# First attention of a two-layer kernel: the last products of a block in four pieces among the next block's scores and transposes, and the queries scaled by ScalarE

## The chip, the cores and the metric

The kernel runs on one core of one Trainium2 chip. The metric is the device time of one execution in microseconds; the figure to beat is the median of three runs.

## What is computed

There are two layers, each an attention and a mixture of experts, on x of shape (4, 512, 256) in float32. The change touches only the first attention of layer 0. For each of the four batches ("blocks" here), with e the layer-normed rows of x, q the 1024 context rows, and w1, w2, w3 thirds of a weight vector, it is

```
Sim  = (e @ w1)[:, None] + (q @ w2)[None, :] + (e * w3) @ q.T + b
A    = softmax(Sim, axis=1)                 # 512 x 1024
hq   = A @ q                                # 512 x 256
Batt = softmax(max(Sim, axis=1), axis=0)
hc   = Batt @ e                             # one row of 256, the same for all rows
x   += concat([e, hq, e * hq, e * hc]) @ W_qv + b_qv
```

After it come, per block, the routing of the 512 rows to the experts (a layer norm, logits, the two best experts, a place for each row, indirect stores of the rows), then the experts' tiles, then layer 1. The kernel computes (e * w3 + w2) @ q.T in one product, and leaves out what a softmax cancels.

## The kernel before, in words

**Tiling.** A block's 512 rows are four tiles t of 128 rows. `sim_norm` is the layer norm (VectorE, and one square root on ScalarE). `sim_prep` (L273) transposes the normed rows with TensorE into two PSUM tiles `eTp` (one for each half c of the 256 columns), copies each to `eT`, and makes the scaled queries `q0T`. `sim_scores(t)` (L297) makes a 128x1024 score tile `s` in PSUM with L301, its negated row maximum on VectorE (L307), the exponential on ScalarE into `p` (L251), and the division by the row sum on VectorE (L253, L254). `turn_probs(t)` (L257) transposes `p` in eight pieces into two PSUM tiles `a0t` (L261); VectorE copies the first to `a0T` (L265), ScalarE the second (L267).

**The end of a block.** `sim_finish` is a generator in pieces. `attend(0)` and `attend(1)` are the products `hq` over `a0T` (L331), each evicted by ScalarE (`hqT`, L334) and then VectorE (`ehT`, L335). Then comes the row `hc` (L350, L352), and the products of W_qv with `hqT` and `ehT` for tiles 0 and 1 (`hcq`, L367). Its last piece turns the row `hc` (`hcc`, L379), builds the weights `weff` from it on VectorE (L385), does the products with `weff` for the four tiles, those of tiles 2 and 3 together with their `hqT` and `ehT` products, and adds each tile to x on VectorE (L392).

**Order.** TensorE runs the program order, written out by hand in `layer0_attention`: while block b is finished, the scores and transposes of block b+1, the preparation of block b+2 and the routing of block b-1 (`route_steps`: norm L784 to L804, transposes L235, logits `lgT` L834, `lg` L843 and the choice of experts up to `rt_cnt` L852, places `pos` L860 and L861 up to `rt_posi` L874, stores `rows` L894) are put between the pieces. The order on VectorE, ScalarE and GpSimd is chosen by a planner when the kernel is built; each engine then runs its own list in order.

**Buffers.** Three PSUM pools hold two buffers each: score tiles, transposes (`ps_t`: `eTp`, `a0t`, `g`, `hc`, `hcc`, `gb` and others), products (`ps_m`: `hq`, `hcq`, `lgT`, `lg`, `pos`, `k`, `v`). A buffer is written again only after its last reader. In SBUF the pool `k4` has twelve buffers of 4 KB per partition, for `xn`, `eT`, `q0T`, `p`, `hqT`, `ehT` and others. Its first tile is `zeros`, the source of nine transfers that clear the buffers in DRAM (20.6 MB written), issued by GpSimd (L194 and L201).

**After the attention.** TensorE goes on with keys and values of layer 1 (`k` L475, `v` L489) while block 3 is routed (its normed rows are `rowbuf`), and then with the experts' tiles.

Of the kernel before, what the change touches and what calls it, by code (L numbers as in the profile page):

```python
# [12 lines left out]
AF = mybir.ActivationFunctionType  # L13
ALU = mybir.AluOpType
# [3 lines left out]
P = 128  # L18
NB = 4
S = 512  # L20
NT = S // P
M = 1024
NJ = M // P
D = 256
# [36 lines left out]
def two_layers(ctx: ExitStack, tc: tile.TileContext, io, out):  # L61
# [75 lines left out]
    def after(a, b, why):  # L137
        info = mybir.DependencyInfo(mybir.DependencyClass.Sync, mybir.DependencyReason.DATA)
        tc.add_manual_dep(a.ins, b.ins.name, info, reason=why)
# [10 lines left out]
    x = []  # L150
# [3 lines left out]
    def load_ctxn(b):  # L154
        t = t8([P, NJ, D], f"ctxn_{b}")
        nc.sync.dma_start(out=t, in_=io["ctx"][b].rearrange("(j p) d -> p j d", p=P))
        ctxn[b] = t
# [98 lines left out]
    def turn_probs(dst, p, t, name):  # L256

        for g in range(2):
            pt = tr_ps(f"{name}_{g}")
            for j in range(4):  # L260
                nc.tensor.transpose(pt[:, bass.ts(j, P)], p[:, bass.ts(4 * g + j, P)], ident)  # L261
            d = dst[:, 4 * g : 4 * g + 4, bass.ts(t, P)]
            s = pt.rearrange("p (j n) -> p j n", n=P)
            if g == 0:
                nc.vector.tensor_copy(d, s)  # L265
            else:
                nc.scalar.copy(d, s)  # L267
# [5 lines left out]
    def sim_prep(st):  # L273
        b, xn = st["b"], st["xn"]
        eT = t4([P, NC, S], f"eT_{b}")
        qT = t4([P, NC, S], f"q0T_{b}")
        for c, pt in transposed(xn, f"eTp_{b}"):
            nc.vector.tensor_copy(eT[:, c, :], pt)
            st["scaled"] = nc.vector.tensor_scalar(  # L279
                qT[:, c, :], eT[:, c, :], wsim[:, 2, c : c + 1], wsim[:, 1, c : c + 1], ALU.mult, ALU.add  # L280
            )
        nc.gpsimd.tensor_tensor(x[b], x[b], bqv.unsqueeze(1).to_broadcast([P, NT, D]), ALU.add)
        st.update(eT=eT, qT=qT, negmax=tsmall([P, NT], "s0_negmax"))

    def sim_rows(st):
# [10 lines left out]
    def sim_scores(st, t):  # L296
        b = st["b"]  # L297
        sp = score_ps(f"s0_{b}_{t}")
        for c in range(NC):
            for h in range(2):  # L300
                nc.tensor.matmul(  # L301
                    sp[:, h, :], st["qT"][:, c, bass.ts(t, P)], ctxT[b][:, c, bass.ts(h, 512)],
                    start=(c == 0), stop=(c == NC - 1),
                )
        spf = sp.rearrange("p h n -> p (h n)")
        nm = st["negmax"][:, t : t + 1]
        nc.vector.tensor_reduce(nm, spf, AX.X, ALU.max, negate=True)  # L307
        p = t4([P, M], f"p0_{b}_{t}")
        softmax_exp(p, spf, 1.0, nm)
        return p  # L310

    def sim_finish(st):

        b, xn, eT, aT = st["b"], st["xn"], st["eT"], st["aT"]

        mx = tsmall([P, NT], "b0_mx")
        nc.vector.scalar_tensor_tensor(mx, st["r"], bsim, st["negmax"], ALU.add, ALU.subtract)
        m1 = tsmall([P, 1], "b0_m1")
        nc.vector.tensor_reduce(m1, mx, AX.X, ALU.max)
        gp = tr_ps(f"g0_{b}")  # L320
        nc.tensor.transpose(gp[0:1, 0:P], m1, ident)
        g = tsmall([1, 1], "b0_g")
        nc.vector.tensor_reduce(g, gp[0:1, 0:P], AX.X, ALU.max, negate=True)

        hq = t4([P, NC, S], f"hqT_{b}")
        eh = t4([P, NC, S], f"ehT_{b}")

        def attend(c):
            op = mm_ps(f"hq_{b}_{c}")
            for j in range(NJ):  # L330
                nc.tensor.matmul(  # L331
                    op, ctxn[b][:, j, bass.ts(c, P)], aT[:, j, :], start=(j == 0), stop=(j == NJ - 1)
                )
            nc.scalar.copy(hq[:, c, :], op)  # L334
            st["attended"] = nc.vector.tensor_tensor(eh[:, c, :], op, eT[:, c, :], ALU.mult)  # L335

        attend(0)
        yield
        bp = tr_ps(f"gb0_{b}")
        nc.tensor.matmul(bp[:, 0:1], ones[0:1, :], g, start=True, stop=True)  # L340
        gb = tsmall([P, 1], "b0_gb")
        nc.vector.tensor_copy(gb, bp[:, 0:1])
        eb = tsmall([P, NT], "b0_eb")
        es = tsmall([P, 1], "b0_es")
        nc.scalar.activation(eb, mx, AF.Exp, bias=gb, accum_out=es)
        attend(1)
        yield

        hp = tr_ps(f"hc0_{b}")
        nc.tensor.matmul(hp[0:1, D : D + 1], es, ones[:, 0:1], start=True, stop=True)  # L350
        for t in range(NT):
            nc.tensor.matmul(  # L352
                hp[0:1, 0:D], eb[:, t : t + 1], xn[:, t, :], start=(t == 0), stop=(t == NT - 1)
            )
        rt = tsmall([1, 1], "b0_rt")
        nc.vector.reciprocal(rt, hp[0:1, D : D + 1])
        hr = sm.tile([1, D], F32, tag="b0_hr", name=f"b0_hr_{b}", bufs=1)
        nc.vector.tensor_scalar(hr, hp[0:1, 0:D], rt, None, ALU.mult)
        ops = {}

        def products(t, k, last):
            if not last:
                ops[t] = mm_ps(f"hcq_{b}_{t}")[:, 0:D]
            op = ops[t]
            for c in range(NC):
                for i, (l, w) in enumerate(k):
                    nc.tensor.matmul(  # L367
                        op, l[:, c, bass.ts(t, P)], w(c), start=(not last and c == 0 and i == 0),
                        stop=(last and c == NC - 1),
                    )  # L370

        late = [(hq, lambda c: wqv[:, 2 + c, :]), (eh, lambda c: wqv[:, 4 + c, :])]
        for t in range(2):
            products(t, late, False)
        yield

        hp = tr_ps(f"hcc0_{b}")
        for c in range(NC):
            nc.tensor.matmul(hp[:, c : c + 1], hr[:, bass.ts(c, P)], ones[0:1, 0:1], start=True, stop=True)  # L379
        hc = tsmall([P, NC], "b0_hc")  # L380
        nc.vector.tensor_copy(hc, hp[:, 0:NC])

        weff = sm.tile([P, NC, D], F32, tag="weff", name=f"weff_{b}", bufs=1)
        for c in range(NC):
            nc.vector.scalar_tensor_tensor(  # L385
                weff[:, c, :], wqv[:, 6 + c, :], hc[:, c : c + 1], wqv[:, c, :], ALU.mult, ALU.add
            )
        for t in range(NT):
            if t >= 2:
                products(t, late, False)  # L390
            products(t, [(eT, lambda c: weff[:, c, :])], True)
            nc.vector.tensor_tensor(x[b][:, t, :], ops[t], x[b][:, t, :], ALU.add)  # L392

        yield

    def layer0_attention():


        st, ps = {0: sim_norm(0)}, {}

        def scores(b, t):
            ps[t] = sim_scores(st[b], t)

        def turns(b, t):
            if t == 0:
                st[b]["aT"] = tbig(f"a0T_{b}")
            turn_probs(st[b]["aT"], ps.pop(t), t, f"a0t_{b}_{t}")

        def step():
            if route is not None:  # L410
                next(route)

        sim_prep(st[0])
        st[1] = sim_norm(1, st[0]["scaled"])
        load_ctxn(1)
        scores(0, 0)
        scores(0, 1)
        sim_rows(st[0])
        turns(0, 0)
        scores(0, 2)  # L420
        turns(0, 1)
        scores(0, 3)
        sim_prep(st[1])
        turns(0, 2)
        turns(0, 3)
        route = None
        for b in range(NB):
            more = b + 1 < NB
            fin = sim_finish(st[b])
            next(fin)  # L430
            if b + 2 < NB:
                st[b + 2] = sim_norm(b + 2, st[b]["attended"])
            step()
            if more:
                scores(b + 1, 0)
            next(fin)
            step()
            if more:
                scores(b + 1, 1)
            next(fin)  # L440
            if more:
                turns(b + 1, 0)
            next(fin)
            step()
            if more:
                sim_rows(st[b + 1])
                scores(b + 1, 2)
                turns(b + 1, 1)
                scores(b + 1, 3)
                if b + 2 < NB:  # L450
                    load_ctxn(b + 2)
                    sim_prep(st[b + 2])
            step()
            if more:
                turns(b + 1, 2)
                turns(b + 1, 3)
            route = route_steps(L0, b)
            next(route)
        return route
# [941 lines left out]
```

## Time and profile before

| | us |
|---|---|
| median of 3 runs | 987.43 (987.35 to 987.92) |
| profiled execution, whole | 984.93 |
| span of the profiled execution | 982.9 |
| TensorE busy | 902.5 (92%) |
| VectorE busy | 439.6 (45%) |
| ScalarE busy | 328.7 (33%) |
| GpSimd busy | 227.1 (23%) |
| mean granted TensorE clock | 0.971 of full speed |

The first attention with its routing fills about the first 246 us of the span. The profile's lines read: start, length, engine, line of the kernel, operation, output and inputs by the program's names, count, and in brackets the idle time of that engine just before, with what released it. TensorE's ends are modelled, so that the starts are the safer numbers.

### The profile page before, as it was taken

What the parts mean: (1) busy time and instruction counts of PE and PEld (TensorE: products, weight loads), DVE (VectorE), ACT (ScalarE), POOL (GpSimd) and SP (SyncE); (2) the same over time, 40 slices, a digit from 0 to 9 for tenths busy, and PEclk for the clock granted to TensorE, in tenths of its full rate; (3) what the DMA queues carried; (4) which work ended last, traced back from release to release, by engine and by line L of the source; (5) the groups of instructions that cost most, each with busy time, mean ns of one, the idle gap of its engine ahead of it and who ended that gap; (6) DMA issues with size and microseconds to landing.
All of it is one profiled execution on the core that took longest, in us unless ns stands there. A gap on an engine that the chain in (4) does not pass through costs nothing.

```text
span 982.9 us, 15181 instructions
## 1 busy us (share of the span) xinstructions
PE 902.5 (92%) x5506; PEld 672.3 (68%) x5506; DVE 439.6 (45%) x1262; ACT 328.7 (33%) x727; POOL 227.1 (23%) x275
## 2 busy tenths in 40 slices
PE   5888999988989999989989989989899999999995
PEld 2445464645569899546656655656778999999995
DVE  6455474544732322665664765756461211112110
ACT  2222221221111111365673464555332322323321
POOL 3310103040512222000130141133642112221121
PEclk9898999989999999999999999999989999999998
DMA  9999901211139797600000111220325868578971
GB/s 317 288 259 236 284 2 34 84 51 43 46 93 303 227 298 272 222 22 2 23 1 1 29 49 62 90 98 23 108 81 150 277 198 270 175 238 269 292 243 19
DMA packets 54907, 142.05 MB, mean 145 GB/s; under 512 B 6775, under 2 KB 32814, under 8 KB 48681
## 3 DMA queue, kind: packets, MB, share of 16 engines
q1 hardware_dynamic: 39144, 102.89, 31.4%
q0 software_dynamic: 15392, 38.10, 15.2%
q8 instruction: 47, 0.77, 0.3%
q14 instruction: 36, 0.29, 0.1%
q10 hardware_dynamic: 288, 0.00, 0.0%
HBM read 131.51 MB, written 39.91 MB: 174 GB/s over the span
## 4 chain that ended last, share of the span: by engine, by line
PE 46%; DVE 4%; ACT 4%; issue 4%; DMA 1%; another core or an unknown queue 0%; POOL 0%; POOLq 0%; ACTq 0%; DVEq 0%
PE hp L1085 11%; PE y L1110 10%; PE s L587 6%; PE a2t L610 5%; PE o L635 4%; DVE p L596 2%; ACT p L600 2%; PE y_ahead L1110 2%; PE hp_ahead L1085 1%; DMA out<-yw,to 1%; PE q L571 1%; PE v L489 1%; PE k L475 1%; PE b L934 1%; PE lgT L834 1%
## 5 line engine op out<-in xcount | busy, mean ns | idle before, releaser
L1094 ACT ACTIVATE aT<-hp,w1s 128x128 f32<-128x128 f32 x248 | 67.6, 383 | 159.2 <-issue 159.2
L1085 PEld LDWEIGHTS hp<-hT,w1s 128*128 128x128 f32 x992 | 115.6, 192 | 3.5 <-DVE hT L1066 1.9
L1085 PE MATMUL hp<-hT,w1s 128*128 128x128 f32 x992 | 116.2, 275 | 1.4 <-DVE hT L1066 1.4
L1110 PE MATMUL y<-w2s,aT 128*128 128x256 f32 x496 | 112.0, 379 | 0.0
L596 DVE CUSTOM_DVE_ANT_0 p<-s,mbias 128x1024 f32<-128x1024 f32 x64 | 75.8, 1221 | 54.0 <-PE s L587 53.9
L1110 PEld LDWEIGHTS y<-w2s,aT 128*128 128x128 f32 x496 | 91.9, 190 | 11.2
L600 ACT ACTIVATE p<-p,s_nm 128x1024 f32<-128x1024 f32 x64 | 73.5, 1148 | 66.1 <-DVE s_nm L596 66.1
L1127 POOL DMA_INDIRECT out<-yw,to x31 | 47.8, 1542 | 178.2 <-DVE to L1051 90.6
L610 PEld LDWEIGHTS a2t<-ident,p 128*128 128x128 f32 x512 | 56.9, 143 | 44.9 <-issue 22.1
L1114 DVE TENSOR_SCALAR yw<-y,row 128x256 f32<-128x256 f32 x59 | 28.6, 484 | 125.4 <-PE y L1110 125.4
L610 PE MATMUL a2t<-ident,p 128*128 128x128 f32 x512 | 72.8, 283 | 12.2 <-ACT a2T L615 5.8
L894 POOL DMA_INDIRECT rows<-rowbuf,rt_posi x64 | 65.2, 1019 | 77.5 <-DVE rt_posi L874 19.7
L587 PE MATMUL s<-kT,q2T 64*128 64x512 f32 x256 | 68.9, 642 | 2.1 <-DVE s_nm L596 2.1
L635 PE MATMUL o<-a2T,v 128*64 128x128 f32 x1024 | 63.3, 276 | 1.7 <-ACT kT L480 1.1
L331 PE MATMUL hq<-a0T,ctxn 128*128 128x512 f32 x128 | 63.0, 649 | 0.5 <-DVE a0T L265 0.5
L635 PEld LDWEIGHTS o<-a2T,v 128*64 128x64 f32 x1024 | 55.4, 137 | 11.5 <-issue 7.5
L615 ACT COPY a2T<-a2t 128x512 f32<-128x512 f32 x96 | 53.7, 581 | 23.0 <-PE a2t L610 22.7
L301 PE MATMUL s<-ctxT,q0T 128*128 128x512 f32 x128 | 59.8, 613 | 0.5 <-DVE q0T L279 0.5
L1066 DVE TENSOR_SCALAR hT<-ht,w1s 128x128 f32<-128x128 f32 x62 | 22.6, 406 | 81.7 <-PE ht L1060 76.0
L1085 PEld LDWEIGHTS hp<-hT,w0s 128*128 128x128 f32 x448 | 54.2, 192 | 3.3 <-DVE hT L1062 2.0
L1085 PE MATMUL hp<-hT,w0s 128*128 128x128 f32 x448 | 54.8, 276 | 1.1 <-DVE hT L1062 1.0
L1110 PE MATMUL y<-w0s,aT 128*128 128x256 f32 x224 | 52.8, 379 | 0.0
(259 smaller groups left out, 1245.7 us busy)
## 6 DMA issues: line engine op xcount, KB each, us to landing
w1s<-in_w1p SPq DMA_DIRECT2D x34, 1030.0 KB
w2s<-in_w2p SPq DMA_DIRECT2D x34, 1024.0 KB
rows<-zeros POOLq DMA_DIRECT2D x8, 2064.0 KB
w0s<-in_w1p SPq DMA_DIRECT2D x31, 512.0 KB
w0s<-in_w2p SPq DMA_DIRECT2D x31, 512.0 KB
row<-rows SPq DMA_DIRECT2D x59, 129.0 KB
ctxT<-in_ctxT SPq DMA_DIRECT2D x4, 1024.0 KB
ctxn<-in_ctx SPq DMA_DIRECT2D x4, 1024.0 KB
```

What stands on the lines that cost most here:

```text
L301: nc.tensor.matmul(sp[:, h, :], st["qT"][:, c, bass.ts(t, P)], ctxT[b][:, c, bass.ts(h, 512)], start=(c == 0), stop=(c == NC - 1),)
L331: nc.tensor.matmul(op, ctxn[b][:, j, bass.ts(c, P)], aT[:, j, :], start=(j == 0), stop=(j == NJ - 1))
L587: nc.tensor.matmul(sps[r][:, k, :], st["qT"][at, n, bass.ts(t, P)], st["kT"][at, n, bass.ts(k, 512)], start=True, stop=True,)
L596: nc.vector.tensor_tensor_reduce(p, sps[r].rearrange("p h n -> p (h n)"), st["mbias"][:, t, :], -ATT_SCALE, -ATT_SCALE * LEAST, ALU.add, A ...
L600: nc.scalar.activation(p, p, AF.Exp, bias=nm, scale=-1.0, accum_out=tot[:, r : r + 1])
L610: nc.tensor.transpose(pt[:, bass.ts(j, P)], p[:, bass.ts(4 * g + j, P)], ident)
L615: nc.scalar.copy(d, pt)
L635: nc.tensor.matmul(op[r * HD : r * HD + HD, :], st["v"][:, j, bass.ts(2 * n + r, HD)], aT[:, r, bass.ts(j, P)], start=(j == 0), stop=(j == ...
L894: i = nc.gpsimd.indirect_dma_start(out=rows[:, :], out_offset=bass.IndirectOffsetOnAxis(ap=pos_i[:, k, t : t + 1], axis=0), in_=buf[:, k, ...
L1085: nc.tensor.matmul(o, w1[:, c * ff + f * P : c * ff + f * P + P], hT[:, c, :], start=(c == 0), stop=(c == NC - 1),)
L1094: nc.scalar.activation(aT[:, f, :], hp[:, f // 4, bass.ts(f % 4, P)], AF.Gelu_apprx_tanh, bias=w1[:, at : at + 1])
L1110: nc.tensor.matmul(op, aT[:, f, :], w2[:, f * D : f * D + D], start=(f == 0), stop=(f == nf - 1))
```

## The change

In `sim_prep` the scaled queries are made by ScalarE from the PSUM tile, not by VectorE from `eT`; GpSimd's addition of b_qv to x now comes after the last of these. In `sim_finish` the last piece becomes four: the row and the weights `weff`; the final products of tiles 0 and 1; those of tile 2; those of tile 3. In `layer0_attention` the scores of block 1's tile 0 come before block 0's last transposes; in every block the scores (b+1, 2) come between the piece that makes `weff` and the first final products; the transposes (b+1, 1) and the scores (b+1, 3) come before the products of tiles 2 and 3; and the preparation of block b+2 and the transposes (b+1, 2) come after these.

```diff
         for c, pt in transposed(xn, f"eTp_{b}"):
-            nc.vector.tensor_copy(eT[:, c, :], pt)
-            st["scaled"] = nc.vector.tensor_scalar(
-                qT[:, c, :], eT[:, c, :], wsim[:, 2, c : c + 1], wsim[:, 1, c : c + 1], ALU.mult, ALU.add
+            st["scaled"] = nc.vector.tensor_copy(eT[:, c, :], pt)
+            scaled = nc.scalar.activation(
+                qT[:, c, :], pt, AF.Identity, bias=wsim[:, 1, c : c + 1], scale=wsim[:, 2, c : c + 1]
             )
-        nc.gpsimd.tensor_tensor(x[b], x[b], bqv.unsqueeze(1).to_broadcast([P, NT, D]), ALU.add)
+        i = nc.gpsimd.tensor_tensor(x[b], x[b], bqv.unsqueeze(1).to_broadcast([P, NT, D]), ALU.add)
+        after(i, scaled, "not beside VectorE's copies")
...
                 weff[:, c, :], wqv[:, 6 + c, :], hc[:, c : c + 1], wqv[:, c, :], ALU.mult, ALU.add
             )
+        yield
         for t in range(NT):
...
             nc.vector.tensor_tensor(x[b][:, t, :], ops[t], x[b][:, t, :], ALU.add)
-
-        yield
+            if t > 0:
+                yield
...
         turns(0, 2)
+        scores(1, 0)
         turns(0, 3)
...
             step()
-            if more:
+            if more and b > 0:
                 scores(b + 1, 0)
...
             next(fin)
+            if more:
+                scores(b + 1, 2)
+            next(fin)
             step()
             if more:
                 sim_rows(st[b + 1])
-                scores(b + 1, 2)
                 turns(b + 1, 1)
                 scores(b + 1, 3)
-                if b + 2 < NB:
-                    load_ctxn(b + 2)
-                    sim_prep(st[b + 2])
+            next(fin)
+            next(fin)
+            if b + 2 < NB:
+                load_ctxn(b + 2)
+                sim_prep(st[b + 2])
+            if more:
+                turns(b + 1, 2)
             step()
             if more:
-                turns(b + 1, 2)
                 turns(b + 1, 3)
```

One consequence for the routing: `step()`, which for b > 0 runs a piece of the routing of block b-1, keeps its place after the piece that holds tiles 0 and 1. So `lg` and the choice of experts of block b-1 now come before the products of tiles 2 and 3, and `pos` after them. For the last block nothing of a next block stands between the pieces.

More of the change, by code (lines that the diff above doesn't have):

```diff
@@ L401, in scores @@
         def scores(b, t):
-            ps[t] = sim_scores(st[b], t)
+            ps[b, t] = sim_scores(st[b], t)
         def turns(b, t):
@@ L406, in turns @@
                 st[b]["aT"] = tbig(f"a0T_{b}")
-            turn_probs(st[b]["aT"], ps.pop(t), t, f"a0t_{b}_{t}")
+            turn_probs(st[b]["aT"], ps.pop((b, t)), t, f"a0t_{b}_{t}")
         def step():
```

## The prediction

> **What bounds the kernel now.** I read the page's busy shares first: TensorE is busy 92% of the span, so idle TensorE is what can be won. Its slices:
>
> ```profile
> PE   5888999988989999989989989989899999999995
> PEclk9898999989999999999999999999989999999998
> DMA  9999901211139797600000111220325868578971
> ```
>
> The first ten slices (246 us) hold the first attention. There TensorE has idle tenths and the granted clock dips, while DMA is full until slice 5. The chain of waits reaches back only to 396 us, to the end of the first experts, so it says nothing of this stage. I therefore took the timeline of TensorE, in order of time, and looked for waits:
>
> ```profile
> 72.12 3.68 PE L367 MATMUL hcq<-weff,eT 128*128 128x256 f32 x8 [3.37 <-DVE weff L385]
> ...
> 129.84 1.99 PE L367 MATMUL hcq<-weff,eT 128*128 128x256 f32 x8 [0.77 <-DVE weff L385]
> ...
> 203.68 1.06 PE L261 MATMUL a0t<-ident,p 128*128 128x128 f32 x8 [2.89 <-DVE p L254]
> ...
> 206.27 10.06 PE L331 MATMUL hq<-a0T,ctxn 128*128 128x512 f32 x16 [0.47 <-DVE a0T L265]
> ...
> 245.31 0.42 PE L860 MATMUL pos<-rt_cnt,before 128*128 128x48 f32 x2 [3.87 <-DVE rt_cnt L852]
> ```
>
> TensorE waits for `weff` in each block (0.77 us; 3.37 in block 0, where GpSimd adds to x at 69.33), for the last `p` of block 3, and for the choice of experts. After a longer wait the work itself is slow: the 10.06 us of `hq` are 7.03 at 151.79. The windows show why:
>
> ```profile
> 205.28:208.70 3.42, 2.81 (x4) 0.51 0.15 54
> 208.70:212.10 3.40, 3.40 (x5) 0.50 0.23 80
> 246.24:249.65 3.41, 3.41 (x5) 0.51 0.00 0
> ```
>
> Columns: window, length, TensorE busy (count), granted clock, DMA. The clock is half for one or two windows of 3.41 us.
>
> One thing in this stage is not bound by TensorE. The exponential of tile 1 of block 2:
>
> ```profile
> 121.77 1.23 DVE L307 TENSOR_REDUCE s_negmax<-s 128x1 f32<-128x1024 f32 x1 [2.89 <-PE s L301]
> ...
> 124.51 1.11 ACT L251 ACTIVATE p<-s,s_negmax 128x1024 f32<-128x1024 f32 x1 [7.60 <-DVE s_r L291]
> ```
>
> Its maximum was done at 123.0, yet it began at 124.51. The order of ScalarE, in both kernels, lists all eight GpSimd DMA semaphores at this instruction: its `p` gets the buffer of `zeros`, so **it waits until the clearing transfers have landed**. DMA share falls from 0.42 (121 to 122 us) to 0.07 in the next us.
>
> [...] clock 0.50, all changes on a grid of 3.41 us, and windows with 1.55 us of work or less were followed by half clock (89.23 to 92.64), one with 2.19 (147.25) was not. [...] `ehT` at 47.83 starts as `hqT` ends (47.80). So `q0T` on ScalarE waits for VectorE's copy of the same bank; the order of waits of the changed kernel shows it. [...] no table load stands before `q0T` in the new order.
>
> **The change part by part.** The orders of both kernels show that after the first attention all five engines' lists are the same, so what TensorE gains by 246 us should pass to the end unless a transfer is bound to absolute time.
>
> *Queries on ScalarE.* Removes 8 scalings from VectorE (0.55 us at 9.77), adds 8 on ScalarE; priced by the eviction `hqT` of the same shape, 0.59. VectorE's copy still comes first (0.69), so the first scores start at 10.37 as before; at each later `eTp` the buffer is free 0.6 us later than by the copy alone. The bounds of the unseen instruction are 0.59 and 0.7. GpSimd's additions come after ScalarE: block 1's now behind the clears in its queue, about 69 us, block 3's at about 147. Nobody needs them before 70 and 225 us. No DMA issue of SP moves.
>
> *Blocks 0 and 1 up to `hcc` of block 1.* Scores of 3.43 us now cover `weff` (0.88 alone), and block 1's first scores cover the wait for block 0's last `p` (2.07 at 36.18). With them go half-clock windows (3.68 against 1.99 at 72.12; 8.99 against 7.03 at 95.61). By replaying the new orders with these durations I have TensorE about 11 us earlier by then, before `hcc` near 117 instead of 128.47. **This is not kept.** VectorE's list has the reciprocal and scaling of the gated `p` ahead of the copy `a0T` that frees the PSUM buffer of `hcc`. The clears are not earlier: same issues, full DMA. So: exponential 124.51, end 125.75 with its accumulator read, reciprocal 0.15, scaling 0.75, copy 0.69: `hcc` at 127.3. **Gain 1.15.**
>
> *Restart.* TensorE then stood for some 10 us, so it restarts at half clock: between one window (1.7 us lost) and two (3.4); middle 2.5. **-2.5.** No such row before had this long a wait.
>
> *Rest of block 1.* `hcc` to the first final products was 1.37; now `hcc` to scores 0.45: +0.9. The transposes before `hq` (L331) waited 0.95, 0.68, 0.29 and 0.67 (3.5 between starts). Now `q0T` frees the first at +1.05, and the last waits for ScalarE's table load 1.28 and root 0.30 ahead of its copy: 2.25. **Net +2.1.**
>
> *Block 2.* `weff` +1.1 as above. The wait for the last `p` of block 3 (2.89, then 0.68 and 0.47; 4.5 between starts) goes, since 5.2 us of products of tiles 2 and 3 lie between its scores and its transposes; what comes next late is VectorE's two copies, 0.55. **+5.0**, and `hq` of block 3 begins near 200 with a filled window before it, so 7.03 for 10.06: **+3.0.**
>
> *Block 3.* `lg` comes 5.2 us earlier, before the products of tiles 2 and 3; the choice chain (241.48 to 245.25) fits beside them. The 3.87 goes, and `k` follows warm (5.2 between starts against 3.45): +5.7. New: the `rowbuf` of block 3 is now late. VectorE's list has places (1.8), four additions to x (1.67) and four normalisations (4 x 0.41) after the last product, against 3.45 us of `k`: TensorE waits about 2.0 before L235. **+3.7.** ScalarE also gets a table load (1.28) ahead of block 3's expert weights, beside VectorE's chain to `rt_cnt` (260.16 to 261.83): 0 to 0.3, taken as 0.
>
> Sum 1.15 - 2.5 + 2.1 + 5.0 + 3.0 + 3.7 = 12.45, say **12.5 us** off the profiled 984.93 (span 982.9 and 2.0 around it). That execution is 2.5 below the median of 987.43; I find no place for that, so I take the same 12.5 off the median: **974.9**. A difference of 0.2% (2 us) is about what a measurement can tell.
>
> **Rivals.**
> - *The clock falls again.* With waits of 2.2 us before `hq` of block 2 a window may have too little work (the trace stayed warm with 2.19 busy, fell with 1.55), and `hq` of block 3 may stay slow. Cost 2.2 and 3.0: gain 7.3, 980.1. For it: half-clock windows come in pairs (205.28). Against: the products ahead fill the windows. 0.16.
> - *No gate.* If the clears do not hold TensorE, the 11 us stay and no restart is paid: gain 12.5 + 9.9 + 2.5 = 24.9, 962.5. Against: the semaphores in the order, and the full DMA. 0.04.
> - *Not what it says: swallowed later.* GpSimd's queue of stores, or its additions, set the experts' start. Block 2's stores take 8 x 1.29 and now end near 245, block 3's begin near 251; 6 us of room. If the room fails, only the 1.15 of `hcc` is left: 986.3. 0.05.
> - *Slower: the gate closes later.* GpSimd's last clear is issued at 67.74, after an earlier one has landed. Were the clears delayed, each us goes straight to the end, since VectorE and TensorE are stopped behind one exponential. They would decide from 12.5 us on (landing after 137); at 141 they cost 16.5, so 991.4. Against: DMA does the same work. 0.05.
>
> **How the numbers follow.** The main case 0.70, its range 972 to 978 (restart 1.7 or 3.4, the wait before L235 from 0.5 to 3, `q0T` 0.59 to 0.7). To reach 8 in 10 I go up to the clock's case: 971.5 to 981.5. Faster: 0.70 + 0.16 + 0.04 = 0.90; same 0.05; slower 0.05.
>
> **What would show it.** In the changed profile: no wait for `weff` in blocks 0 to 2; a TensorE gap of about 10 us that ends near 127 in `hcc`, behind an exponential that starts at 124 to 125; `hq` of block 3 near 200, 7 us long; `pos` without its 3.87; a new wait of about 2 us for `rowbuf` before L235. Wrong if `hcc` comes at 117, if the experts' first tile is not some 12 us earlier, or if `hq` of block 3 is again 10 us.

## The result and the profile after

The changed kernel took **976.47 us** (median of 4 runs, 970.82 to 977.04) against 987.67 (987.35 to 989.21) for the kernel before on the same chip: a ratio of 0.9871, 95% interval 0.9845 to 0.9897. The profiled execution took 976.42 (span 974.6) against 984.93 (982.9). Lines of the changed kernel from L283 on are one higher than before, from L395 on eight higher: `s` is L302, `hq` L332, `hcq` L368, `hcc` L380, `weff` L386, `pos` L868.

The granted clock in the slices of the page, changed kernel:

```profile
PEclk9999989999999999999999999979899999999998
```

The three dips of the clock in the first nine slices are gone, and a new one stands in the sixth (122 to 146 us). Later there is a 7 in the slice from 633 to 658 us and an 8 from 682 to 707; the kernel before had one 8 there, from 713 to 737. The timeline of TensorE, first three more lines of the kernel before, then the changed kernel at the places shown of before:

```profile
127.09 1.04 PE L261 MATMUL a0t<-ident,p 128*128 128x128 f32 x8
128.47 0.60 PE L379 MATMUL hcc<-ones,b_hr 1*128 1x1 f32 x4 [0.35 <-DVE a0T L265]
...
285.71 2.05 PE L1085 MATMUL hp<-hT,w0s 128*128 128x128 f32 x16 [0.52 <-DVE hT L1062]
```

```profile
72.31 1.99 PE L368 MATMUL hcq<-weff,eT 128*128 128x256 f32 x8 [0.56 <-DVE weff L386]
...
118.82 1.04 PE L261 MATMUL a0t<-ident,p 128*128 128x128 f32 x8
126.99 1.01 PE L380 MATMUL hcc<-ones,b_hr 1*128 1x1 f32 x4 [7.13 <-DVE a0T L265]
127.93 5.25 PE L302 MATMUL s<-ctxT,q0T 128*128 128x512 f32 x8
...
146.91 1.33 PE L261 MATMUL a0t<-ident,p 128*128 128x128 f32 x8 [1.16 <-ACT q0T L279]
...
150.27 7.03 PE L332 MATMUL hq<-a0T,ctxn 128*128 128x512 f32 x16
...
199.88 7.03 PE L332 MATMUL hq<-a0T,ctxn 128*128 128x512 f32 x16
...
232.24 0.32 PE L868 MATMUL pos<-rt_cnt,before 128*128 128x48 f32 x2
...
237.12 0.33 PE L235 MATMUL xn0rTp<-ident,rowbuf 128*128 128x128 f32 x1 [0.50 <-DVE rowbuf L812]
...
238.93 1.88 PE L483 MATMUL k<-ctxT,wkv 128*128 128x512 f32 x4
...
272.92 2.05 PE L1093 MATMUL hp<-hT,w0s 128*128 128x128 f32 x16 [0.52 <-DVE hT L1070]
```

TensorE was 8.3 us earlier at 118.82 (127.09 before), stood still for 7.13 us, and went on at 126.99 (128.47 before): an early gain, thrown away. What it stood behind is in the timeline of ScalarE, changed kernel:

```profile
123.94 1.11 ACT L251 ACTIVATE p<-s,s_negmax 128x1024 f32<-128x1024 f32 x1 [15.30 <-DMA ys<-zeros]
```

The profile itself now names the clearing transfer as the releaser. From there to the `k` behind L235 every stage is as long as before or shorter. Each row of this table is the difference between two starts, of before and after; the sums run to the experts' first `hp` (285.71 before, 272.92 after), my mark for the end of the changed stage. `k` behind L235 is the first product of the keys after the transposes of block 3's `rowbuf`.

| from, to | before | after | gain | predicted |
|---|---|---|---|---|
| start to `hcc` of block 1 | 128.47 | 126.99 | 1.48 | 1.15 |
| to `hq` of block 2 | 23.32 | 23.28 | 0.04 | -2.5 + 2.1 |
| to `hq` of block 3 | 54.48 | 49.61 | 4.87 | 5.0 |
| to `k` behind L235 | 45.59 | 39.05 | 6.54 | 3.0 + 3.7 |
| to the experts' `hp` | 33.85 | 33.99 | -0.14 | 0 |
| to the end of the span | 697.2 | 701.7 | -4.5 | 0 |

The last row is where this execution lost part of it again. After `hp` the lists of all engines are the same in both kernels, and the gain is held for 350 us: the transposes at 631.93 before start at 619.48 after, 12.45 earlier. Then the second attention, first before and then after:

```profile
651.39 2.52 PE L587 MATMUL s<-kT,q2T 64*128 64x512 f32 x8
```

```profile
639.32 3.79 PE L595 MATMUL s<-kT,q2T 64*128 64x512 f32 x8
```

The same eight records take 3.79 us instead of 2.52, and at a `wo` behind them (662.88 before, 653.70 after) the gain is 9.18. From the transposes to this `wo` TensorE is busy for 30.90 us instead of 27.63 and idle for 3.32 in both, so that all of the loss there is slower work. The windows say why; their columns are the window, its length, then for each engine its busy time and count, then granted clock, DMA share and GB/s. Before, then after, at the same products:

```profile
653.10:654.80 1.70, 1.70 (x12) 0.86 (x8) 0.85 (x1) 0.00 (x0) 0.00 (x0) 1.00 0.00 0
```

```profile
641.10:642.80 1.70, 1.70 (x6) 0.34 (x2) 0.00 (x0) 0.00 (x0) 0.00 (x0) 0.50 0.00 0
```

TensorE is busy throughout in both and the clock is half in one. Over the whole span the time at half clock comes in pieces of 3.41 us or multiples (read in windows of 0.85 us). Before `hp` there are **nine such pieces in the kernel before and four after**, and each costs at most half its length, 1.7 us; between `hp` and the last 30 us there are six and, in this execution, eight.

### The profile page after: what moved, and what is told of

Same layout as the page of the kernel before. It is cut to its first block, busy times and chain, and to the rows that moved or that the text cites. A ratio compares the mean times of both kernels' runs of the same rounds, so it can differ in the third digit from the quotient of the medians.

```text
span 974.6 us, 15175 instructions
## 1 busy us (share of the span) xinstructions
PE 898.3 (92%) x5506; PEld 670.2 (69%) x5506; DVE 431.6 (44%) x1254; ACT 331.6 (34%) x733; POOL 226.1 (23%) x275
## 4 chain that ended last, share of the span: by engine, by line
PE 46%; DVE 5%; ACT 4%; issue 3%; DMA 1%; another core or an unknown queue 0%; POOL 0%; POOLq 0%; ACTq 0%; DVEq 0%
PE hp L1093 11%; PE y L1118 10%; PE s L595 6%; PE a2t L618 5%; PE o L643 4%; DVE p L604 2%; PE y_ahead L1118 2%; ACT p L608 2%; DMA out<-yw,to 1%; PE q L579 1%; PE v L497 1%; PE hp_ahead L1093 1%; PE k L483 1%; PE lgT L842 1%; PE wo L658 1%
## 5 line engine op out<-in xcount | busy, mean ns | idle before, releaser
L1118 PEld LDWEIGHTS y<-w2s,aT 128*128 128x128 f32 x496 | 91.9, 190 | 11.2
L302 PE MATMUL s<-ctxT,q0T 128*128 128x512 f32 x128 | 63.3, 642 | 0.7 <-ACT q0T L279 0.7
L332 PE MATMUL hq<-a0T,ctxn 128*128 128x512 f32 x128 | 56.8, 596 | 0.1
```

Of the source, the lines that this page charges most:

```text
L302: nc.tensor.matmul(sp[:, h, :], st["qT"][:, c, bass.ts(t, P)], ctxT[b][:, c, bass.ts(h, 512)], start=(c == 0), stop=(c == NC - 1),)
L332: nc.tensor.matmul(op, ctxn[b][:, j, bass.ts(c, P)], aT[:, j, :], start=(j == 0), stop=(j == NJ - 1))
L1118: nc.tensor.matmul(op, aT[:, f, :], w2[:, f * D : f * D + D], start=(f == 0), stop=(f == nf - 1))
```

## The experiments

Twelve kernels ran in three sets of four; a set shared one chip and the runs of the kernel before on it (medians 983.55, 983.8 and 987.87). The marks are starts in each kernel's profiled execution; the ratio is to the kernel before, with its 95% interval; "half" counts the pieces of 3.41 us at half clock before `hp`.

| kernel | `hcc` of block 1 | first `hp` | half | `hp` to end | median | ratio |
|---|---|---|---|---|---|---|
| own_zeros | 118.81 | 261.20 | 1 | 694.2 | 958.22 | 0.9752 (0.9719 to 0.9784) |
| before_own_zeros | 128.56 | 285.82 | 9 | 693.8 | 981.70 | 0.9978 (0.9957 to 0.9998) |
| order_alone | 127.31 | 273.69 | 5 | 697.6 | 971.13 | 0.9863 (0.9837 to 0.9889) |
| scaling_alone | 128.66 | 285.23 | 9 | 696.4 | 985.61 | 1.0031 (1.0014 to 1.0048) |
| after_again | 123.30 | 267.37 | 3 | 693.4 | 965.75 | 0.9858 (0.9806 to 0.9910) |
| hq_twice | 143.85 | 287.96 | 5 | 697.6 | 984.23 | 1.0013 (0.9994 to 1.0033) |
| late_choice | 122.26 | 269.54 | 3 | 697.3 | 971.14 | 0.9895 (0.9854 to 0.9937) |
| q_from_copy | 121.88 | 264.85 | 3 | 694.0 | 961.76 | 0.9793 (0.9744 to 0.9841) |
| pieces_together | 119.27 | 266.59 | 2 | 696.4 | 966.43 | 0.9818 (0.9764 to 0.9871) |
| weff_bare | 126.53 | 270.61 | 3 | 696.3 | 966.74 | 0.9799 (0.9746 to 0.9852) |
| own_zeros_no_early | 118.39 | 262.51 | 2 | 697.1 | 961.82 | 0.9761 (0.9722 to 0.9799) |
| order_own_zeros | 120.36 | 264.07 | 2 | 696.8 | 960.31 | 0.9725 (0.9671 to 0.9780) |

In what follows "the gate" is the exponential that is held until the clearing transfers have landed, with what stands behind it. My theory was that waits of TensorE taken away behind the gate make the gain, and that what is won ahead of it is swallowed. Its first rival was that the scaling by ScalarE brings the gain; its second, that every early us passes to the end.

### The gate: own_zeros and before_own_zeros

```diff
-    zeros = t4([P, ROW], "zeros")
+    zeros = sm.tile([P, ROW], F32, tag="oT", name="zeros", bufs=1)
```

The same edit in the changed kernel and in the kernel before. The tag `oT` belongs to a small buffer of the second attention.

> The changed kernel, with `zeros` in a buffer of the pool of small tiles that nobody else uses before the second attention; orders of all engines unchanged, the exponential of p_2_1 no longer waits for the clears. Theory (gate): hcc of block 1 comes 1.38 us after the transposes begin at 118.82, so at 120.2 instead of 126.99, and the scores after it take 3.7 us instead of 5.25; the experts' first hp is then some 8.5 us earlier than 272.92, at 264.4, and the total about 968. Rival (early time is lost elsewhere, for example to the loads or to VectorE): hcc stays at 126 to 127 and the total at 976. A second rival: row stores wait for the clears and give part back; then hp at 267 to 270.

> The kernel before, with `zeros` in its own buffer. Theory (gate): in the kernel before, the exponential of p_2_1 is held for 1.5 us only (maximum done at 123.0, start at 124.51), and TensorE has products up to 128.1, so hcc of block 1 stays at 128.5, the experts' first hp at 285.7 and the total within 1 us of 987.4. Rival (the clears cost both kernels alike, as traffic or as a wait): as large a gain here as in the changed kernel with the same edit, 8 us, to 979.

TensorE's timeline in own_zeros:

```profile
118.81 0.60 PE L380 MATMUL hcc<-ones,b_hr 1*128 1x1 f32 x4 [0.35 <-DVE a0T L265]
119.34 3.70 PE L302 MATMUL s<-ctxT,q0T 128*128 128x512 f32 x8
...
261.20 2.05 PE L1093 MATMUL hp<-hT,w0s 128*128 128x128 f32 x16 [0.52 <-DVE hT L1070]
```

The 7.13 us and the slow scores are gone together, with the order of instructions unchanged. **The gate is shown.** `hp` came 3.2 us earlier than I expected. 1.4 of it lie in block 0 (`hq` of block 1 at 87.91 against 89.30), 1.7 are a half-clock piece at 267 to 271 us that the changed kernel has and this one has not. In the kernel before the same edit left `hcc` and `hp` where they were (128.47 and 285.71); the ratio of 0.9978 is a gain of 2 us (0.2 to 4), which the marks of the stage do not show, and not the 8 of the rival. Taking `zeros` out of the pool can also give its later tiles other buffers; nothing of that shows at the marks of this control. In these two kernels the clears cost time only where TensorE is early enough to wait for them: 7.13 us in the changed one.

### Which part of the change: order_alone and scaling_alone

order_alone is the changed kernel with `sim_prep` as before; scaling_alone is the kernel before with the new `sim_prep`:

```diff
-            st["scaled"] = nc.vector.tensor_copy(eT[:, c, :], pt)
-            scaled = nc.scalar.activation(
-                qT[:, c, :], pt, AF.Identity, bias=wsim[:, 1, c : c + 1], scale=wsim[:, 2, c : c + 1]
+            nc.vector.tensor_copy(eT[:, c, :], pt)
+            st["scaled"] = nc.vector.tensor_scalar(
+                qT[:, c, :], eT[:, c, :], wsim[:, 2, c : c + 1], wsim[:, 1, c : c + 1], ALU.mult, ALU.add
             )
...
-        after(i, scaled, "not beside VectorE's copies")
```

> The changed kernel with the queries scaled by VectorE again from the copied rows, and GpSimd's addition to x free of the wait; the new order stays. Theory (order and gate): most of the gain stays, the experts' first hp at 272 to 275, total 976 to 979; hcc of block 1 at 127. Rival (ScalarE's scaling is what brings the gain): hp at 284 or later, total 986 to 988.

> The kernel before, with only the queries scaled by ScalarE and GpSimd's addition put behind them; the old order stays. Theory (order and gate): no more than 1.5 us either way: hp at 284.2 to 287, total 986 to 989. Rival (ScalarE's scaling is what brings the gain): hp at 273 to 276, total 976 to 979.

The order alone makes the whole gain: its ratio cannot be told from the changed kernel's. The scaling alone costs 0.3% in the medians (0.1 to 0.5). The timeline of TensorE in scaling_alone shows a price, the wait of the transposes for the PSUM buffers of `eTp`, 0.95 in the kernel before:

```profile
148.78 3.58 PE L261 MATMUL a0t<-ident,p 128*128 128x128 f32 x16 [2.03 <-ACT q0T L279]
```

From `hcc` of block 1 to `hq` of block 2 this took 24.56 us instead of 23.32. At `hp` nothing of it is left (285.23 against 285.71), since `hq` of block 3 was less slow (8.56 us for 10.06). What makes the 0.3% is therefore not shown. The first rival is out.

### The largest term: pieces_together

```diff
             next(fin)
+            if b == 2:
+                next(fin)
+                next(fin)
             step()
...
-            next(fin)
-            next(fin)
+            if b != 2:
+                next(fin)
+                next(fin)
```

> The changed kernel with `zeros` in its own buffer, so that no gate blurs the comparison, and in block 2 alone the products of tiles 2 and 3 put back before block 3's last scores, directly behind tiles 0 and 1, as in the kernel before. Theory: the wait for the last p of block 3 is back (2.9, then 0.7 and 0.5, less the 0.35 now there): hcc of block 2 to hq of block 3 takes 22.4 us instead of 18.71 (171.04 to 189.75), and hq after it is slow (8.5 to 10 us instead of 7.03); the experts' first hp comes 3.7 to 6.7 us later than 261.2, counted from hcc of block 1 at 118.81. Rival (TensorE would not have waited, the gain of block 2 comes from weff alone): 18.7 to 19, hp unchanged.

TensorE's timeline:

```profile
191.96 1.53 PE L261 MATMUL a0t<-ident,p 128*128 128x128 f32 x8 [3.07 <-DVE p L254]
...
194.29 7.79 PE L332 MATMUL hq<-a0T,ctxn 128*128 128x512 f32 x16
```

From `hcc` of block 2 (171.50) to `hq` of block 3 it took 22.79 us against 18.71, with one more half-clock piece at 192.0 to 196.3 that fell on the transposes more than on `hq`: `hq` took 7.79 us, less than the 8.5 to 10 expected. From `hcc` of block 1 to `hp` it took 147.32 against 142.39 in own_zeros: 4.9 us, within 3.7 to 6.7. **The cover of block 3's last p is shown**, wait and clock together.

### The choice of block 3: late_choice

The changed kernel with this edit; for the last block the two `next(fin)` now stand ahead of `step()`:

```diff
             next(fin)
+            if not more:
+                next(fin)
+                next(fin)
             step()
...
                 scores(b + 1, 3)
-            next(fin)
-            next(fin)
+                next(fin)
+                next(fin)
```

> The changed kernel with one place of the order undone: in block 3 (and only there) the products of tiles 2 and 3 come before the products lg and the choice of experts, as in the kernel before. Theory: the wait of pos for rt_cnt (3.87) is back and k after it is slow; from 226.37 on, lg is 5.2 us later, pos comes at about 236.1 instead of 232.24, the waits for rowbuf (0.74) go, so L483's k after the transposes starts 3.7 us later, at 242.6, hp at 276.6, total 3.7 us longer. Rival (the choice is hidden anyway, the gain of block 3 is its faster hq alone): no change, hp at 273.

TensorE's timeline in late_choice:

```profile
122.26 0.60 PE L380 MATMUL hcc<-ones,b_hr 1*128 1x1 f32 x4 [3.15 <-DVE a0T L265]
...
229.16 0.42 PE L871 MATMUL pos<-rt_cnt,before 128*128 128x48 f32 x2 [3.88 <-DVE rt_cnt L863]
...
269.54 2.05 PE L1096 MATMUL hp<-hT,w0s 128*128 128x128 f32 x16 [0.52 <-DVE hT L1073]
```

The absolute starts expected for it are not met, because in this set the gate opened sooner (next experiment). Counted from `hcc`, `hp` takes 147.28 against 144.07 in after_again on the same chip: 3.2 us longer, 3.7 expected. The wait of 3.88 is back, with half clock from 229.5 to 233.8. The step holds; the ratios (0.9895 and 0.9858) have the right distance, but their intervals overlap.

### What the gate swallows: after_again and hq_twice

after_again is the changed kernel itself. hq_twice repeats block 0's products:

```diff
-            for j in range(NJ):
+            for _ in range(2 if b == 0 else 1):
+              for j in range(NJ):
```

> The changed kernel unaltered, for comparison on the same chip as the three runs beside it. Both theories: ratio to the kernel before of 0.985 to 0.99, the experts' first hp at 272.5 to 273.5. If the half-clock windows of the late stages fall by chance, as the difference between executions of this kernel suggests, the total may differ by 2 to 6 us with hp at the same place.

> The changed kernel, with the 16 products hq of block 0 computed twice over: 7.1 us more work for TensorE ahead of the clears' gate, nothing else changed and the output the same. Theory (gate): TensorE was idle for 7.13 us before hcc of block 1, so hcc stays at 127 to 127.5; the window before it is now full, so the scores after it take 3.7 us instead of 5.25, and the experts' first hp comes at 271.3 to 273, no later than the 272.92 of the changed kernel; total the same within 2 us. Rival (every us of TensorE ahead of hcc passes to the end): hp at 280, total 7 us longer.

**The expectation of hq_twice was missed, and the kernel does not test what it was made for.** Two faults were mine. A product of float32 shows as two records, so a row of x16 is one `attend` of 8 products, and the edit added 14.1 us (two rows of 14.0 instead of 7.1), not 7.1. And the longer lines shifted the choice of buffers: now `ehT` of block 1 got the buffer of `zeros`, as the order's list of waits shows, and VectorE stood still there. VectorE's timeline in hq_twice:

```profile
119.24 0.69 DVE L337 TENSOR_TENSOR ehT<-hq,eT 128x512 f32<-128x512 f32 x1 [10.63 <-issue]
```

The releaser reads "issue", that is, nothing that the profile connects; the list of waits and the time name it (the clears landed at 119.21 in late_choice, on the same chip). A third reason is when the clears landed. TensorE's timeline in after_again:

```profile
71.43 0.60 PE L380 MATMUL hcc<-ones,b_hr 1*128 1x1 f32 x4 [2.67 <-DVE a0T L265]
...
123.30 0.60 PE L380 MATMUL hcc<-ones,b_hr 1*128 1x1 f32 x4 [0.35 <-DVE a0T L265]
...
267.37 2.05 PE L1093 MATMUL hp<-hT,w0s 128*128 128x128 f32 x16 [0.52 <-DVE hT L1070]
```

In this set the clears landed about 4.7 us sooner (the gated exponential began at 119.21 in late_choice, at 123.94 in the changed kernel's first profile), while TensorE was 3.9 us later at `hcc` of block 0 (71.43 against 67.52). So TensorE did not wait at the gate at all, and `hp` was 5.5 us earlier than in the first profile. The place of `hp` that was expected for after_again, 272.5 to 273.5, was missed by this. Beside it hq_twice was 15.0 us later at `hcc` of block 0 and 20.6 later at `hcc` of block 1 and at `hp`. The 5.5 between the two lie behind the held `ehT`, in TensorE's timeline of hq_twice:

```profile
122.58 0.49 PE L342 MATMUL gb<-b_g,ones 1*128 1x1 f32 x2 [3.83 <-ACT xn0rT L245]
```

ScalarE had to wait for VectorE there, and VectorE stood behind `ehT`. So this run does not test the swallowing; that rests on own_zeros and its control. It does show that the gate moves with the buffer to whichever tile inherits it.

### The weights: weff_bare

```diff
             next(fin)
-            if more:
-                scores(b + 1, 2)
             next(fin)
+            if more:
+                scores(b + 1, 2)
             step()
```

> The changed kernel with `zeros` in its own buffer, and in every block the next block's scores of tile 2 put back behind the final products of tiles 0 and 1, so that these again follow hcc directly. Theory: TensorE waits for weff again, 0.77 us in blocks 1 and 2 (0.8 to 3.4 in block 0, where GpSimd adds to x beside VectorE): hcc of block 1 to hq of block 2 takes 22.2 us instead of 21.32, hcc of block 2 to hq of block 3 19.6 instead of 18.71; hp 2.6 to 5 us later in all. Rival (the wait is only moved, the scores then stand where TensorE had to wait for p): 21.3 and 18.7, hp unchanged.

TensorE's timeline:

```profile
73.68 3.52 PE L368 MATMUL hcq<-weff,eT 128*128 128x256 f32 x8 [4.35 <-DVE weff L386]
...
127.90 1.99 PE L368 MATMUL hcq<-weff,eT 128*128 128x256 f32 x8 [0.77 <-DVE weff L386]
```

Block 2 has the same wait of 0.77 at 180.97. Blocks 1 and 2 met the expectation to a few hundredths: 22.17 us from `hcc` to the next `hq` (22.2 expected), and 19.56 (19.6). Block 0 was under-estimated: `hcc` of block 0 (68.73) to `hq` of block 1 (95.63) took 26.90 against 20.96, and a half-clock piece stands behind the wait of 4.35 (`hcq` took 3.52 us there). So `hp` came 9.4 us later than in own_zeros, not 2.6 to 5: 1.8 were there at `hcc` of block 0 already, 5.9 are block 0, 1.7 blocks 1 and 2. **The cover of weff is shown** by these marks. The early 5.9 us are worth something only without the gate: the gate took 7.13 us of TensorE's time in the changed kernel.

### Block 0's early scores: own_zeros_no_early

```diff
         turns(0, 2)
-        scores(1, 0)
         turns(0, 3)
...
-            if more and b > 0:
+            if more:
                 scores(b + 1, 0)
```

> The changed kernel with `zeros` in its own buffer, and block 1's first scores put back from ahead of block 0's last transposes to behind its first hq, as in the kernel before. Theory: without the gate this place counts: the wait for block 0's last p (2.07 us) comes back, hcc of block 0 at about 69 instead of 66.95, hp 2 us later and, if a half-clock window comes with the wait, up to 5.5 later. Rival (the early scores wait for the queries themselves and gain nothing): hp within 0.5 of 261.2.

The rival was right about the place. `hcc` of block 0 came at 66.53, 0.4 earlier than in own_zeros, and the wait of 2.07 is not back: TensorE's timeline has the last two tiles' transposes in one row.

```profile
34.51 3.41 PE L261 MATMUL a0t<-ident,p 128*128 128x128 f32 x16 [2.35 <-ACT q0T L279]
```

TensorE waits there for the scaled queries, and this covers the wait for the last `p`. The later `hp` (262.51 against 261.20, where the rival had said within 0.5) has a half-clock piece at 256.8 to 261.1 that own_zeros has not. This move of the change gains nothing here.

### A better version: q_from_copy and order_own_zeros

Both stand on own_zeros. The first lets ScalarE read VectorE's copy, the second is `sim_prep` as before:

```diff
-                qT[:, c, :], pt, AF.Identity, bias=wsim[:, 1, c : c + 1], scale=wsim[:, 2, c : c + 1]
+                qT[:, c, :], eT[:, c, :], AF.Identity, bias=wsim[:, 1, c : c + 1], scale=wsim[:, 2, c : c + 1]
```

> The changed kernel with `zeros` in its own buffer, and ScalarE scaling the queries from VectorE's copy eT in SBUF instead of from PSUM: the PSUM buffer of the transposes is free after the copy alone. Theory (the PSUM buffer is held by both readers in turn): the waits of 1.16 us of the transposes of p for q0T fall to about 0.55 in blocks 1 and 2, hp comes about 1.2 us before the 261.2 of the kernel with its own zeros, total 1.2 us shorter (a ratio to the kernel before of about 0.974). Rival (the transposes wait for the second copy or for ScalarE's table load behind it anyway): hp within 0.3 us of 261.2.

> The changed kernel with `zeros` in its own buffer and the queries scaled by VectorE again from the copied rows: the new order without ScalarE's part and without the gate. Theory: the transposes of p wait 0.35 us instead of 1.16 for the copies of the transposed rows in blocks 1 to 3; hcc of block 1 to the experts' first hp takes about 141 us instead of 142.4; total the same as with ScalarE's scaling or 1 us less, a ratio to the kernel before of 0.974 (so ScalarE's part brings nothing by itself). Rival (VectorE is short of time and its scalings delay TensorE): 144 us or more, ratio 0.978 or more.

TensorE's timeline, in q_from_copy and then in order_own_zeros:

```profile
87.92 1.26 PE L261 MATMUL a0t<-ident,p 128*128 128x128 f32 x8 [0.35 <-DVE eT L278]
```

```profile
137.53 1.25 PE L261 MATMUL a0t<-ident,p 128*128 128x128 f32 x8 [0.35 <-DVE eT L278]
...
139.45 1.09 PE L261 MATMUL a0t<-ident,p 128*128 128x128 f32 x8 [0.30 <-ACT a0T L267]
...
141.22 0.27 PE L321 MATMUL g<-ident,b_m 128*1 128x128 f32 x1 [0.68 <-ACT a0T L267]
```

In both the wait of 1.16 fell to 0.35; 0.55 or so was expected for q_from_copy. In q_from_copy the stretches from `hcc` to the next `hq` became shorter by it, 19.73 and 20.23 us in blocks 0 and 1 against 20.96 and 21.32 in own_zeros. In order_own_zeros they took 20.68 and 20.97: there the next waits, for the copies to `a0T` (0.30 and 0.68), took most of it back. At `hp` nothing came of it. From `hcc` of block 1 on q_from_copy took 142.97 and order_own_zeros 143.71 (141 expected, 144 or more by the rival) against 142.39. Both have one half-clock piece there that own_zeros has not (259.4 and 258.6 on); without its 1.7 us they would be 1.1 and 0.4 shorter. And `hcc` of block 0 came at 71.25 in q_from_copy, 4.3 later than in own_zeros, so that the `hp` expected for it, 260, was missed by some 5 us. The ratios of the three kernels overlap. **own_zeros is faster than both kernels of the case** by their ratios; whether ScalarE or VectorE scales makes no difference that these runs can tell.

## Why the prediction was right, point by point

The forecast was 974.9 in 971.5 to 981.5; 976.47 was measured. The sum of the stage was 12.45; at the same place, `k` behind L235, 12.93 were measured (251.86 to 238.93). That the total fell within 1.6 us of the forecast is partly luck: the part behind `hp`, which the change does not touch, took 701.7 us here and 693.4 in after_again, and one of the four runs, 970.82, lies outside the range.

- **The gate, +1.15.** Measured 1.48, by the mechanism named: exponential at 123.94 (124 to 125 said), `hcc` at 126.99 (127.3 said). The idle time is 7.13, not some 10: TensorE came 8.3 us early, not 11. Missing are early waits that I set too low: in block 0 the transposes at 34.47 waited 2.35 for `q0T` (1.30 for `eT` before), so that `hcc` of block 0 came only 0.63 earlier. One cause is the length of `q0T`: 0.59, at most 0.7, was priced by `hqT` (0.586 in both kernels), and 0.777 measured (median of eight, 0.768 to 0.778). The first one began at 9.86, as VectorE's copy from the same PSUM tile ended (9.83), and the first scores accordingly started at 10.69, not "at 10.37 as before". All this was swallowed by the gate.
- **No wait for weff in blocks 0 to 2.** Wrong in block 0, where 0.56 stayed: scores of 3.70 did not cover a `weff` that took 4.30 (two instructions in VectorE's timeline at 68.35) instead of 0.88. I had read the 3.37 of before as GpSimd's doing and then counted `weff` "alone". The timeline of VectorE, then of GpSimd, changed kernel:

```profile
68.35 4.30 DVE L386 SCALAR_TENSOR_TENSOR weff<-wqv,b_hc 128x256 f32<-128x256 f32 x2
```

```profile
67.94 1.65 POOL L201 DMA_DIRECT2D ys<-zeros  x1 [20.57 <-issue]
69.53 2.43 POOL L282 TENSOR_TENSOR x<-x,bqv 128x1024 f32<-128x1024 f32 x1
```

  `weff` ends 0.7 us after GpSimd does (72.65 and 71.96), and block 1's took 0.88 in the kernel before (129.31). That GpSimd's work held it is my estimate from these times; no run here takes the two apart.
- **The restart, -2.5.** Measured 1.96: `hcc` 1.01 for 0.60 and the scores 5.25 for 3.70. Within 1.7 to 3.4.
- **The rest of block 1, +2.1.** 0.04 + 1.96 = 2.0.
- **Block 2, +5.0.** 4.87, and pieces_together shows the larger part of it (4.08). The 1.1 that I took for `weff` "as above" is 0.9 by the working above it (1.37 less 0.45); with that the sum is 4.85.
- **The faster hq of block 3, +3.0.** 10.06 to 7.03, as said.
- **Block 3, +3.7.** 6.54 - 3.03 = 3.5. Its new wait shows in brackets as 0.50 and 0.24 only. From the start of `k` (232.92) to L235 it is 4.20 instead of 3.45, though, and L235 to the next `k` is 1.81 instead of 0.87: 1.7 together, 2.0 said; the parts that I listed (1.8, 1.67 and four times 0.41, less 3.45) also give 1.7. And 3.87 with the 1.75 of `k` is 5.6, not 5.7.
- **"What TensorE gains by 246 us should pass to the end".** This step failed in part: 12.8 us at `hp` became 8.3 at the end of the profiled span, 11.2 in the medians. Of the 4.5 us between, 3.0 are the same 4652 records of TensorE done slower (655.47 us busy before, 658.46 after) and 1.5 are idle time. No transfer took the 3.0: the half-clock pieces of the second attention fell differently in this execution. In after_again the same program needs 693.4 us from `hp` on, 8.3 less than in the first profile; and one of the four runs of the changed kernel took 970.82, with a mean clock of 0.979 against 0.975.

Of the rivals, "the clock falls again" named the right agent in the wrong place: `hq` of block 3 was warm, the second attention was not. "No gate" is what the execution of after_again shows, because TensorE was late and the clears early; late_choice on the same chip still waited 3.15 us at `hcc`. "Swallowed later" and "the gate closes later" did not occur; GpSimd's stores of block 2 ended at 245.2 and block 3's began at 252.12, about as worked out.

What the prediction priced in single terms but did not add up is how much of the gain is clock. The windows from the start to `hp`, with the columns told above; first the kernel before, then the changed kernel:

```profile
0.00:285.70 285.70, 247.05 (x854) 140.28 (x854) 153.64 (x465) 62.67 (x104) 66.51 (x99) 0.95 0.50 145
```

```profile
0.00:272.90 272.90, 239.80 (x854) 136.72 (x854) 145.18 (x457) 65.26 (x109) 65.63 (x99) 0.97 0.53 152
```

TensorE's second figure is its busy time: the same 854 records took 247.05 us and then 239.80. Of the 12.8 us, 7.25 are the same work done faster, and 5.55 are idle time that is gone (38.65 to 33.10). Nine pieces at half clock that became four fit this, at 1.7 us for each in which TensorE is busy throughout. In own_zeros it is one piece, and 235.08 us. No run changed the clock without changing a wait, so that it is the waits that bring the pieces was not tried by itself. Nor does the work in a window decide alone, as the prediction took it to: in the kernel before, on the same grid, windows with 1.85 us of work (at 17.55) and 1.80 (at 655.84) were not followed by half clock, but two with 2.32 (577.34) and 2.64 (645.60), both in the second attention, were. Why stays open.

## What to carry to other kernels

Of every gain ahead of a transfer's landing ask whether anybody later stands behind that landing: here a source tile of 1 KB per partition in a rotating pool stopped two engines. Giving it a buffer of its own was worth as much again as the change (12 us at `hp`, own_zeros against the first profile) where TensorE had waited there, and little where it had not (q_from_copy came 2.5 us before after_again, on one chip). A TensorE wait of about 3 us cost its length here and up to two half-clock pieces of up to 1.7 us behind it (two after the 2.89 us at 203.68 in the kernel before, none after the 3.15 of late_choice), so price a wait together with the granted clock around it. And compare kernels at a mark close behind the edit as well as at the end, because pieces of half clock later in the program moved the end by several us without any change of code (701.7 and 693.4 us from `hp` on).

## What was not expected of the hardware

- The same program ran at 701.7 and at 693.4 us in its unchanged second part, with the granted clock as the visible difference: outside the last slice, the page of the first profile has a 7 from 633 to 658 us and an 8 from 682 to 707, that of after_again an 8 from 624 to 648 and from 697 to 721. The reason is not shown. Half the time at half clock (56.6 of 982.9 us) is 28.3 us, an estimate of what the half clock cost at most, 2.9% of the kernel before.
- The landing of the same clears differed by about 5 us between the sets (exponentials released at 119.21 in late_choice, at 123.94 in the changed kernel's first profile and 124.26 in order_alone). The windows of 5 us show full DMA up to 120 us in the changed kernel's profile, and only 0.48 of it from 115 to 120 in after_again.
- Beside GpSimd's last clear and the addition behind it, one piece of VectorE's work from SBUF to SBUF was long. In after_again (66.19 to 70.21 on GpSimd) it was the division of block 0's `p`, 4.34 us for 0.75, in the changed kernel `weff`, 4.30 for 0.88; in weff_bare TensorE waited 4.35 us for `weff`; in own_zeros `weff` took 0.88 (67.78 to 68.66). The small copy `b_hc` from PSUM was not long: in the changed kernel it took its usual 0.16 us at 68.16, inside the clear's 67.94 to 69.59. Of the 3.9 us by which TensorE was late at 71.43, 2.3 are this wait (2.67 for 0.35); most of the rest is a half-clock piece at 22.2 to 26.5, which the first profile does not have. VectorE's timeline in after_again:

```profile
66.43 4.34 DVE L254 TENSOR_SCALAR p<-p,sx_rt 128x1024 f32<-128x1024 f32 x1
```

- ScalarE's scaling took 0.777 us from PSUM (128x512, with scale and bias read from `wsim`); its eviction `hqT`, of the same shape and also from PSUM, took 0.586.
